# Two graph attention layers on one core: how the last batch's first layer hands over to its second

## The chip, the cores and the metric

The kernel runs on one core of one Trainium2 chip. The metric is the device time of one execution in microseconds (us); lower is better. The engines are named as in the profile: PE is TensorE, DVE is VectorE, ACT is ScalarE, POOL is GpSimd, and SP issues most of the DMA transfers. Each engine works through its own queue of instructions in a fixed order, and semaphores tie the queues together.

## The reference

The input is x, eight batches of 2048 nodes with 256 features in float32, and a 0/1 adjacency matrix of 2048 x 2048 that all batches share. Two layers follow one another; each ends with a residual sum and a normalization over the features:

```
# layer 0: attention in 4 heads of 64, softmax within chunks of 256 keys
q, k, v = x @ Wq.T + bq, x @ Wk.T + bk, x @ Wv.T + bv
scores  = clip(q . k / 8, -10, 10), and -10 where adj == 0
attn    = softmax(scores) over each chunk of 256 keys on its own
ctx     = sum over the 8 chunks of attn @ v
y       = layernorm(ctx @ Wo.T + bo + x) * gamma + beta
x1      = layernorm(x + y)

# layer 1: graph attention in 4 heads of 64
Wh      = x1 @ W
e       = leaky_relu(s_src[i] + s_dst[j], 0.2), masked by adj
h       = elu(softmax_j(e) @ Wh)
out     = layernorm(x1 + h)
```

## The kernel before, in words

**Layer 0.** A batch is worked through in four groups of 512 queries. For each group there are 16 *slots*: two pairs of heads times eight chunks of keys. So a batch has 64 slots, taken two at a time in 32 *pairs* (`p`). In a pair TensorE computes the next pair's scores (`unit`, L422), VectorE clips and masks them out of PSUM (`evict`, L439), ScalarE takes the exponential in place (`exps`, L462), and TensorE multiplies with the values and a column of ones (`product`, L473). ScalarE copies the product to SBUF (L480). `normalize` then divides by the sum: the reciprocal on VectorE (L490), a multiplication on GpSimd (L497), and from the second chunk on an addition to the head pair's sum, also on GpSimd (L499). A finished sum goes to DRAM and comes back turned; only the very last one of a batch is turned by TensorE (`context`, L523, with ScalarE's copy L526).

**Between the layers.** The class `Between` takes a group of 512 rows from its contexts to layer 1's inputs: output projection (L625), addition of the residual (L636), statistics and scaling for a first normalization ("a"), gamma (L642) and a second addition (`again`, L645), and statistics and scaling for a second one ("b"). Of each normalization, the statistics are on VectorE (`stats`, L540 to L549), the power and the offset on GpSimd (L550, L551), and the scaling on ScalarE (L588). The result, x1, is stored to DRAM (`finish`, L650). To be a matmul's weights it must be turned: `load` and `turn` read it back in blocks and transpose these on VectorE (L304, L322); `turn_all` does it with eight TensorE transposes and a copy by ScalarE (L331, L334). `values` projects it (L667). The groups of a batch pass through these steps while later pairs run, by tables that say after which part of which pair each step stands. Groups 2 and 3 of a batch come to their last steps after its last pair.

**Factors.** When all groups of a batch are projected, `factors` makes three pieces (`fs`): the maximum over nodes (L734 to L738), its spread and the exponentials (L742 to L756, of which L755 gives `ed`), and the rows of the source factor, which go through DRAM (L761 to L764), while GpSimd scales the projected values by `ed` in place (L765, L767).

**Layer 1.** The class `Layer1` works in units of 1024 queries and one head, eight to a batch, each with 16 *tiles* of 128 keys, so 128 tiles. `make` writes a tile of weights with one VectorE operation from a row, a column and a mask (L884); `use` multiplies it on TensorE (L913). At a unit's end ScalarE copies the sums (L925), and `close` finishes the unit in stages, one for each call of `rest` (L938 to L957). Masks come from DRAM by SP (L832), five tiles ahead.

**How they are interleaved.** Layer 1 of a batch runs beside layer 0 of the next: `along` is the earlier batch's `Layer1`, and every pair makes and uses four of its tiles. In the last batch (`b + 1 == B`) some tiles of the batch before are held back: from slot `SLOTS - LATE` on, pairs have none, and `step` (close a stage, then make and use two tiles) puts them between the steps of groups 2 and 3 after the last pair. The order in which these stand is a list written by hand (`order`, L1315 to L1319); there is no scheduler. Afterwards the last batch's layer 1 runs alone: its mask is loaded in whole (L798), its row is lifted to PSUM (L825), every third tile is made by ScalarE and GpSimd (L854 to L856), and the finished rows go out.

**Room.** Layer 1's tiles take turns in three buffers (`ep`), the probabilities of layer 0 in six (`prp`). In the last stage VectorE's tiles are in `prp` and the others in `ep`. Products, scores, turned blocks and projections take turns in three double banks of PSUM (`two_banks`).

Of the kernel before, what the change touches and what calls it, by code (L numbers as in the profile page):

```python
# [8 lines left out]
F32 = mybir.dt.float32  # L9
# [8 lines left out]
P = 128  # L18
# [4 lines left out]
def adj_resnorm_kernel(  # L23
# [19 lines left out]
    nc = tc.nc  # L43
# [29 lines left out]
    FIRST = [sum(BANKS[:m]) for m in range(len(BANKS))]  # L73
    TILES = len(UNITS) * NT
    STEP = TILES // SLOTS
    LATE = 18
    WIDE = max(BANKS)
    AHEAD_E = 5
    LEAD = 4
# [401 lines left out]
            raws[s].rearrange("p k i d -> p k (i d)"), pc[:, :, : QT * D1]  # L481
        )

    def normalize(s):

        q, hp, c = where[s]
        raw = raws.pop(s)
        del probs[s]
        rd = small.tile([P, 2, QT, 1], F32, tag="rd", name="rd")
        nc.vector.reciprocal(rd, raw[:, :, :, D:D1])  # L490
        if c == 0:
            accs[q, hp] = small.tile([P, QT, 2, D], F32, tag="acc", name="acc")
        accv = accs[q, hp].rearrange("p t k d -> p k t d")
        part = accv
        if c:
            part = small.tile([P, 2, QT, D], F32, tag="part", name="part", bufs=1)
        nc.gpsimd.tensor_mul(part, raw[:, :, :, :D], rd.to_broadcast([P, 2, QT, D]))  # L497
        if c:
            nc.gpsimd.tensor_add(accv, accv, part)  # L499

    sums = {}

# [273 lines left out]
    class Layer1:  # L776
        def __init__(self, b, gd, waug):
            self.b, self.gd, self.waug = b, gd, waug
            self.made = self.used = 0
            self.rows, self.edge, self.e = {}, {}, {}  # L780
            self.tail = []
            self.alone = b == B - 1
            self.masks = {}
            self.begun, self.lifted = 0, {}
# [74 lines left out]
        def make(self):  # L859

            if self.made == TILES:
                return
            k = self.made
            n, j = k // NT, k % NT
            _, h = UNITS[n]
            if j == NT // 2:
                self.load_row(n + 1)
            self.made += 1
            if not self.alone:
                drip()  # L870
                if j == 0:
                    need(("row", self.b, n))
                self.load_edge(k + AHEAD_E)
                e = ep.tile([P, WIDE * P], F32, tag="e", name="e")
                row = self.rows[n]
            else:
                if j == NT - LEAD:
                    self.lift(n + 1)
                self.make_ahead(k)
                if self.by_pool(k):  # L880
                    return
                e = prp.tile([P, WIDE * P], F32, tag="pr", name="e")
                row = self.lifted[n]
            nc.vector.scalar_tensor_tensor(  # L884
                e,
                row,
                self.gd[:, h, j : j + 1],
                self.mask(k),
                op0=ALU.max,
                op1=ALU.mult,  # L890
            )
            self.e[k] = e
# [261 lines left out]
    for b in range(B):  # L1154
# [6 lines left out]
        for p in range(PAIRS):  # L1161
            s0, s1 = 2 * p, 2 * p + 1
            q, i = p // QP, p % QP
            along = lower if b + 1 < B or s0 < SLOTS - LATE else None
            more = p + 1 < PAIRS
            slow[0] = bool(along) and more
            if not slow[0]:
                drip(len(pieces))

            def hook(now, later):  # L1170
                if group and i in now:
                    now[i](group)
                if before and i in later:
                    later[i](before)

            if p + 2 < PAIRS:
                load_slab(p + 2)
            if i == 0 and q:
                before, group = group, Between(b, q - 1, sd, waug)
            if p == PAIRS - 2 and b + 1 < B:  # L1180
                turns = [project(b + 1, g) for g in range(NCH)]
                turns[0].pop(0)()

            hook(FIRST_OF, {})
            if i == QP - 1 and q > 1:
                turn_context(q, 0)
            if p:
                normalize(s0 - 1)
            if more:
                us = units_of(p + 1)  # L1190
                waiting = burst(p + 1)
                evict(*waiting[0][0], waiting[0][1])
                exps(*us[0])
                exps(*us[1])
            if along:
                along.rest(1)
                along.make()
                along.use()
                along.make()
            else:  # L1200
                if more:
                    evict(*waiting[1][0], waiting[1][1])
                    exps(*us[2])
                if not lower and masks.left():
                    masks.step()
            hook(MIDDLE_OF, NEXT_MIDDLE)
            if closing:
                closing.do(p, "add", "factors")
            if i == 2 and q:
                turn_context(q - 1, 1)  # L1210
            if i == QP - 2 and q < 2:
                turn_context(q, 0)
            product(s0)
            send()
            if closing:
                closing.do(p, "load")
            if i == 1 and q:
                load_context(b, q - 1, 1)
            if i == QP // 2 + 1:
                load_context(b, q, 0)  # L1220
            if along:
                normalize(s0)
                if more:
                    for us_ps in waiting[1:]:
                        evict(*us_ps[0], us_ps[1])
            elif more:
                evict(*waiting[2][0], waiting[2][1])
                exps(*us[3])
            if i == 0 and q:
                send_context(b, q - 1, 1)  # L1230
            if i == QP // 2:
                send_context(b, q, 0)
            if along:
                if more:
                    exps(*us[2])
                along.rest(1)
                along.use()
                along.make()
                along.use()
                along.make()  # L1240
                along.use()
            else:
                normalize(s0)
                if not lower and masks.left() and (p < QP - 2 or p % 2 == 0):
                    masks.step()
            if p == PAIRS - 1:
                if b + 1 < B:
                    turns[0].pop(0)()
                group.again()
            product(s1)  # L1250
            if along and more:
                exps(*us[3])
            hook(LAST_OF, NEXT_LAST)
            hook(FINALLY_OF, NEXT_FINALLY)
            if closing:
                closing.do(p, "sums", "squares", "finish")
        normalize(SLOTS - 1)
        slow[0] = False

        send()  # L1260
# [3 lines left out]

        def begin():
            nonlocal group
            group = Between(b, NCH - 1, sd, waug)

        def ctx():
            context(NCH - 1, 1)  # L1270
# [6 lines left out]
        def start_next():  # L1277
            for us, ps in burst(0):
                evict(*us, ps)

        early = [
            lambda: before.b2.stats(every),
# [20 lines left out]
        if b + 1 < B:  # L1303
            (k0, v0, q0), (l1, t1, k1, v1, q1), (l2, t2, k2, v2, q2), (l3, t3, k3, v3, q3) = turns
            rest = [lambda: lower.rest(1)] if lower else []
            order = [begin, early[0], *rest, l1, k0, ctx, early[2], v0, steps[0], *rest, steps[1], t1, l2, *rest]
            order += [q0, steps[2], early[3], steps[3], l3, k1, *rest, steps[4], v1, early[4], t2, q1]
            order += [steps[5], k2, steps[6], early[5], early[6], steps[7], coming.begin, v2, t3]
            order += [lambda: [load_slab(p) for p in range(2)], steps[8], steps[9]]
            order += [lambda: k3(fs[0]), fs[1], lambda: q2(fs[2]), coming.start, v3, start_next]  # L1310
            order += [lambda: [exps(*us) for us in units_of(0)], q3, coming.make, coming.make]
        else:

            step = lower.step
            order = [begin, early[0], lambda: coming.load_masks(0), step, ctx, early[1], step, steps[0], steps[1], early[2], step]  # L1315
            order += [steps[2], step, steps[3], early[3], step, steps[4], step, steps[5], early[4], step]
            order += [steps[6], early[5], step, steps[7], early[6], step, steps[8], step, steps[9], step]
            order += [fs[0], step, fs[1], step, fs[2], coming.start]
            order += [step] * 5  # L1319
            assert sum(p is step for p in order) == LATE  # L1320
        for piece in order:
            send()
            piece()
# [63 lines left out]
```

## Time and profile before

| what | value |
|---|---|
| median of 3 runs | 3606.09 us (3604.92 to 3607.03) |
| the profiled execution's own time | 3600.65 us |
| its span | 3598.9 us |
| busy: PE, DVE, ACT, POOL | 3505.9, 3037.7, 2300.9, 1430.4 us |
| mean granted TensorE clock | 0.993 |

The span is the time from the first to the last instruction on record; the execution's own time has some 2 us more around it. A row of a group of instructions reads: line, engine, operation, what it writes and reads, the shapes, how often, and in a timeline ahead of this the start and the duration in us. What stands in brackets is how long the engine sat idle just before, and what ended that. In the span's time, the last batch's pairs with tiles end at 3262, its last pair starts at 3341, the last held tile is used up at 3426, and the last stage ends at 3586; some 13 us of closing work follow.

### The profile page before, as it was taken

The numbers are of one execution on the slowest core, as the hardware profiler recorded it, in microseconds if no ns is written. First come the engines' busy times: TensorE is split into PE (matmuls) and PEld (weight loads), VectorE is DVE, ScalarE is ACT, GpSimd is POOL, SyncE is SP. The second block draws the span as 40 slices with busy tenths as digits, with TensorE's granted clock in tenths as the row PEclk, the third lists the DMA queues.
The fourth block names the chain that finished last, engine by engine and source line by source line (L and its number), as shares of the span: only waits on it lengthen the run. The fifth ranks groups of instructions, "written<-read, shape, count | busy, mean of one in ns | idle before, by whom it ended". The sixth has DMA issues, their size and how long they took to land. (4 is left out here: it accounts for less than half of the span.)

```text
span 3598.9 us, 170175 instructions
## 1 busy us (share of the span) xinstructions
PE 3505.9 (97%) x76884; PEld 2611.6 (73%) x76884; DVE 3037.7 (84%) x3652; ACT 2300.9 (64%) x4119; POOL 1430.4 (40%) x1259
## 2 busy tenths in 40 slices
PE   8999999999999999999999999999999999998777
PEld 5666677777777777776777767777677777775677
DVE  5886699977999699996999959998699977996787
ACT  5787556665666566665666657666576666766376
POOL 1555234333333333333443424434343333344366
PEclk9999999999999999999999999999999999999999
DMA  7653333443443444443444344444344443443341
GB/s 177 152 131 81 84 99 101 111 103 103 116 108 103 90 127 109 112 103 88 126 109 103 99 105 126 111 102 99 101 120 108 111 102 105 116 109 78 103 126 38
DMA packets 724072, 386.58 MB, mean 107 GB/s; under 512 B 437264, under 2 KB 683408, under 8 KB 723344
## 3 DMA queue, kind: packets, MB, share of 16 engines
q1 hardware_dynamic: 673344, 342.00, 38.0%
q10 hardware_dynamic: 50000, 33.70, 2.9%
q8 instruction: 601, 9.85, 1.1%
q14 instruction: 127, 1.04, 0.1%
HBM read 318.64 MB, written 56.89 MB: 104 GB/s over the span
## 5 line engine op out<-in xcount | busy, mean ns | idle before, releaser
L462 ACT ACTIVATE pr<-pr 128x1024 f32<-128x1024 f32 x960 | 996.7, 1054 | 443.9 <-DVE pr L439 371.6
L439 DVE SCALAR_TENSOR_TENSOR pr<-ps,slab 128x1024 f32<-128x1024 f32 x960 | 1116.4, 1205 | 106.7 <-PE ps L422 84.8
L884 DVE SCALAR_TENSOR_TENSOR e<-srow,gd,et 128x1024 f32<-128x1024 f32 x896 | 1168.3, 1338 | 13.7 <-PE pa L913 8.6
L913 PEld LDWEIGHTS pa<-waug,e 128*64 128x64 f32 x32768 | 1008.9, 139 | 215.9 <-issue 166.7
L913 PE MATMUL pa<-waug,e 128*64 128x65 f32 x32768 | 1060.8, 224 | 39.8 <-DVE e L884 34.5
L473 PE MATMUL pc<-vaug,pr 128*64 128x65 f32 x30720 | 980.5, 222 | 10.0 <-DVE pr L439 9.7
L497 POOL TENSOR_TENSOR part<-raw,rd 128x512 f32<-128x512 f32 x448 | 476.7, 1064 | 1216.4 <-DVE rd L490 1212.1
L473 PEld LDWEIGHTS pc<-vaug,pr 128*64 128x64 f32 x30720 | 937.6, 138 | 28.7 <-DVE pr L439 25.8
L422 PE MATMUL ps<-qT,kT 64*64 64x512 f32 x8192 | 943.5, 596 | 5.9 <-DVE pr L439 3.3
L422 PEld LDWEIGHTS ps<-qT,kT 64*64 64x64 f32 x8192 | 286.5, 132 | 485.1 <-issue 269.3
L480 ACT COPY raw<-pc 128x520 f32<-128x520 f32 x512 | 302.6, 591 | 484.8 <-PE pc L473 482.2
L499 POOL TENSOR_TENSOR acc<-acc,part 128x512 f32<-128x512 f32 x448 | 587.2, 1311 | 35.2
L490 DVE RECIPROCAL rd<-raw 128x8 f32<-128x8 f32 x512 | 100.9, 197 | 134.0 <-ACT raw L480 127.1
L497 POOL TENSOR_TENSOR acc<-raw,rd 128x512 f32<-128x512 f32 x64 | 66.8, 1043 | 361.6 <-DVE rd L490 361.6
L667 PE MATMUL pw<-w_sb,x1T 128*64 128x264 f32 (+1 forms) x800 | 122.5, 386 | 4.1 <-DVE x1T L322 4.0
L366 PE MATMUL pp<-xT,wk_sb 128*128 128x512 f32 x256 | 118.4, 602 | 2.9 <-DVE xT L322 1.6
L625 PE MATMUL po<-wo_sb,qT 128*64 128x256 f32 (+1 forms) x912 | 120.7, 381 | 0.0
L366 PE MATMUL pp<-xT,wq_sb 128*128 128x512 f32 x256 | 117.4, 598 | 0.0
L949 ACT ACTIVATE sums<-sums,dn 128x64 f32<-128x64 f32 x448 | 117.0, 334 | 0.4 <-ACT y L588 0.4
L382 PE MATMUL pv<-wv_sb,xT 128*128 128x256 f32 x512 | 116.6, 381 | 0.0
L382 PEld LDWEIGHTS pv<-wv_sb,xT 128*128 128x128 f32 x512 | 95.9, 190 | 20.2 <-issue 7.2
L884 DVE SCALAR_TENSOR_TENSOR e<-rowp,gd,et 128x1024 f32<-128x1024 f32 x86 | 103.9, 1272 | 0.6 <-ACT rowp L825 0.6
(140 smaller groups left out, 2505.6 us busy)
## 6 DMA issues: line engine op xcount, KB each, us to landing
et<-edgeD SPq DMA_DIRECT2D x896, 128.0 KB, 2.8
slab<-clipD SPq DMA_DIRECT2D x256, 256.0 KB, 3.8
srow<-rowD SPq DMA_DIRECT2D x256, 128.0 KB, 3.6
xg<-in_x_dram SPq DMA_DIRECT2D x128, 128.0 KB, 3.3
x1D<-y ACTq DMA_DIRECT2D x32, 512.0 KB, 3.0
ctxD<-acc ACTq DMA_DIRECT2D x56, 256.0 KB, 3.4
ctx<-ctxD SPq DMA_DIRECT2D x224, 64.0 KB, 3.0
xp<-in_x_dram SPq DMA_DIRECT2D x224, 64.0 KB, 2.4
```

The lines of the kernel that those rows point to most:

```text
L366: nc.tensor.matmul(pps[c], lhsT=w[:, kc, c * P : (c + 1) * P], rhs=st["xT"][:, kc, :], start=(kc == 0), stop=(kc == KC - 1),)
L382: nc.tensor.matmul(pv[:, u, :], lhsT=st["xT"][:, kc, u * P : (u + 1) * P], rhs=wv_sb[:, kc, :], start=(kc == 0), stop=(kc == KC - 1),)
L422: nc.tensor.matmul(ps[z * D : (z + 1) * D, k, :], lhsT=kT[rows, hp, t * P + z * D : t * P + (z + 1) * D], rhs=qT[rows, hp, cols], start=Tr ...
L439: nc.vector.scalar_tensor_tensor(pr, ps, -CLIP, row.unsqueeze(1).to_broadcast([P, 2, CH]), op0=ALU.max, op1=ALU.min,)
L462: nc.scalar.activation(pr, pr, AF.Exp, scale=0.125)
L473: nc.tensor.matmul(pc[z * D : (z + 1) * D, k, to], lhsT=probs[s][u][:, k, i * P + z * D : i * P + (z + 1) * D], rhs=vaug[:, KT * c + u, 2 ...
L480: nc.scalar.copy(raws[s].rearrange("p k i d -> p k (i d)"), pc[:, :, : QT * D1])
L497: nc.gpsimd.tensor_mul(part, raw[:, :, :, :D], rd.to_broadcast([P, 2, QT, D]))
L499: nc.gpsimd.tensor_add(accv, accv, part)
L667: nc.tensor.matmul(pw[z, k, : F + 2 * H], lhsT=self.x1T[:, c, u * P + z.start : u * P + z.stop], rhs=w1_sb[:, c, :], start=(c == 0), stop= ...
L884: nc.vector.scalar_tensor_tensor(e, row, self.gd[:, h, j : j + 1], self.mask(k), op0=ALU.max, op1=ALU.mult,)
L913: nc.tensor.matmul(self.pa[i // QT][z * D : (z + 1) * D, i % QT, :], lhsT=e[:, i * P + z * D : i * P + (z + 1) * D], rhs=self.waug[:, j, h ...
```

## The change

All of it lies in the last batch. `LATE` goes from 18 slots to 12: pairs 23, 24 and 25 work beside four tiles each, as the pairs before them, and 24 tiles are held instead of 36. In the last pair the group object is created earlier, a tile is made ahead of gamma and another used between the two products, and `normalize` works on VectorE for the last two slots. After the last pair the list is a new one: single `make` (M), `use` (U) and `rest` (R) calls between the steps; group 2's x1 is turned with `turn_all`, so its `load` and `turn` are gone; group 3's addition of beta comes after its first statistics. Held tiles made there are in `prp`.

```diff
-    LATE = 18
+    LATE = 12
...
-    def normalize(s):
+    def normalize(s, engine=nc.gpsimd):
...
-        nc.gpsimd.tensor_mul(part, raw[:, :, :, :D], rd.to_broadcast([P, 2, QT, D]))
+        engine.tensor_mul(part, raw[:, :, :, :D], rd.to_broadcast([P, 2, QT, D]))
         if c:
-            nc.gpsimd.tensor_add(accv, accv, part)
+            engine.tensor_add(accv, accv, part)
...
+            self.room = ep, "e"
...
-                e = ep.tile([P, WIDE * P], F32, tag="e", name="e")
+                pool, tag = self.room
+                e = pool.tile([P, WIDE * P], F32, tag=tag, name="e")
...
+            ending = b + 1 == B and not more
+            if ending:
+                last = Between(b, NCH - 1, sd, waug)
...
+            if ending:
+                lower.make()
             hook(MIDDLE_OF, NEXT_MIDDLE)
...
+            elif ending:
+                lower.use()
+                group.again()
+                normalize(s0, nc.vector)
             else:
                 normalize(s0)
...
-            if p == PAIRS - 1:
-                if b + 1 < B:
-                    turns[0].pop(0)()
+            if p == PAIRS - 1 and not ending:
+                turns[0].pop(0)()
                 group.again()
             product(s1)
...
-        normalize(SLOTS - 1)
+        normalize(SLOTS - 1, nc.gpsimd if b + 1 < B else nc.vector)
...
-            group = Between(b, NCH - 1, sd, waug)
+            group = Between(b, NCH - 1, sd, waug) if b + 1 < B else last
...
-            step = lower.step
-            order = [begin, early[0], lambda: coming.load_masks(0), step, ctx, early[1], step, steps[0], steps[1], early[2], step]
-            order += [steps[2], step, steps[3], early[3], step, steps[4], step, steps[5], early[4], step]
-            order += [steps[6], early[5], step, steps[7], early[6], step, steps[8], step, steps[9], step]
-            order += [fs[0], step, fs[1], step, fs[2], coming.start]
-            order += [step] * 5
-            assert sum(p is step for p in order) == LATE
+            lower.room = prp, "pr"
+            M, U, R = lower.make, lower.use, lambda: lower.rest(1)
+            order = [begin, U, U, ctx, early[0], steps[0], steps[1], early[2], steps[2]]
+            order += [lambda: group.a.stats(every), before.turn_all, lambda: coming.load_masks(0)]
+            order += [group_shift, M, M, U, steps[4], early[5], U, early[6], M]
+            order += [steps[5], U, M, M, R, U, M, U, steps[6], R, steps[7], M, M, U, steps[8], R]
+            order += [U, steps[9], M, R, M, M, U, U, R, fs[0], M, U, fs[1], M, U, fs[2], coming.start]
+            done = sum(p is U for p in order) + 1, sum(p is M for p in order) + 1
+            order += [R, M, U] * (LATE * STEP - done[0])
+            assert LATE * STEP - done[0] >= LATE * STEP - 2 - done[1]
```

In this list `steps` are group 3's steps (bias, output, add, shift with statistics, a scaling, gamma with the second sum and its statistics, b scaling with the store, turn, and twice two blocks of projection), `early` those of group 2 that are left (statistics, nothing, b scaling with the store, load, turn, and twice two blocks of projection), and `fs` the three pieces of the factors.

More of the change, by code (lines that the diff above doesn't have):

```diff
@@ L1279, in start_next, with group_shift @@
                 evict(*us, ps)
+        def group_shift():
+            group.shift()
         early = [
```

## The prediction

> **What bounds the kernel now.** I read the page first. TensorE is busy nearly throughout, so only a stretch in which it idles can be shortened:
>
> ```profile
> PE 3505.9 (97%) x76884; PEld 2611.6 (73%) x76884; DVE 3037.7 (84%) x3652; ACT 2300.9 (64%) x4119; POOL 1430.4 (40%) x1259
> ```
>
> Then busy times by stretch, around the last batch's end. The columns are the stretch, its length, busy us of each engine, granted clock, DMA share, GB/s:
>
> ```profile
> 3262.25:3290.70 28.45, 23.90 (x483) 14.85 (x481) 18.31 (x22) 18.18 (x31) 10.32 (x9) 1.00 0.27 67
> 3346.72:3385.40 38.68, 24.45 (x512) 21.16 (x510) 33.29 (x57) 11.22 (x26) 13.11 (x10) 0.87 0.48 141
> 3385.40:3404.50 19.10, 18.48 (x439) 15.87 (x437) 15.09 (x21) 5.88 (x19) 0.04 (x1) 1.00 0.36 108
> 3404.50:3426.00 21.50, 13.86 (x333) 12.80 (x329) 18.96 (x14) 3.73 (x10) 11.39 (x5) 0.76 0.21 56
> 3426.00:3586.00 160.00, 131.30 (x4096) 128.55 (x4096) 133.42 (x172) 127.83 (x154) 116.79 (x69) 0.94 0.28 86
> ```
>
> The first row is pairs 23 to 25, without held tiles; rows two to four are the stretch with 36 held tiles, where TensorE works 56.8 of 79.3 us; the last is the last batch's second layer alone. TensorE's waits from 3343 to 3426 (us in all, times, longest) name the causes:
>
> ```profile
> PE pa L913 <- DVE e L884: 11.5, 6, 3.6
> PE pt L523 <- POOL acc L499: 6.3, 1, 6.3
> PE pw L667 <- DVE x1T L322: 4.0, 1, 4.0
> ```
>
> The timeline gives the durations. TensorE's score bursts show a pair with four tiles and a pair with none; GpSimd's rows are the last context; the VectorE and GpSimd rows from 3406 on show tiles made while GpSimd scales the weights:
>
> ```profile
> 3249.26 3.66 PE L422 MATMUL ps<-qT,kT 64*64 64x512 f32 x32
> 3262.25 3.66 PE L422 MATMUL ps<-qT,kT 64*64 64x512 f32 x32
> 3271.40 4.00 PE L422 MATMUL ps<-qT,kT 64*64 64x512 f32 x32 [0.18 <-DVE pr L439]
> ...
> 3350.66 2.11 POOL L497 TENSOR_TENSOR part<-raw,rd 128x512 f32<-128x512 f32 x1
> 3352.85 2.12 POOL L499 TENSOR_TENSOR acc<-acc,part 128x512 f32<-128x512 f32 x1
> ...
> 3404.15 0.26 ACT L755 ACTIVATE ed<-sd 128x64 f32<-128x64 f32 x1
> 3405.41 10.48 POOL L767 TENSOR_TENSOR waug<-waug,ed 128x1024 f32<-128x1024 f32 x4
> 3406.45 1.89 DVE L806 TENSOR_SCALAR ngd<-gd 128x64 f32<-128x64 f32 x1
> 3408.26 5.84 DVE L884 SCALAR_TENSOR_TENSOR e<-srow,gd,et 128x1024 f32<-128x1024 f32 x2
> ```
>
> The stretch is set by one chain: last context, output, two normalizations, x1, its projection, the factors (ed ends at 3404.4), the weights' scaling, the last held tiles. Held tiles only fill its gaps.
>
> **What the Trainium skill says.** SBUF — State Buffer, "SBUF: two separate sides": a VectorE operation with two SBUF inputs and a GpSimd operation that reads SBUF exclude each other for a whole instruction. The trace agrees: a tile costs 1.23 us alone and 2.92 beside the scaling. GPSIMD Engine Reference, "3.1 Elementwise": a GpSimd add takes 1.96 times VectorE's at 2048 elements; here L497 and L499 take 1.04 and 1.31 us undisturbed, 2.1 when tiles are made beside them. VectorE: DVE Perf Modes, "The three transpose paths": VectorE turns 32x32 blocks only, TensorE whole squares into PSUM. Here group 3 on TensorE takes 1.09 us and a 1.01 us copy, while group 2 goes through DRAM and needs L322.
>
> **The change, part by part.** Times are on the clock of the run before; its shift comes last.
>
> *Pairs 23 to 25 take four held tiles each.* Pairs with tiles and no extras last 11.21 us (scores at 3083.28 and 3094.49). Three cost 33.63 against 28.45 here, where TensorE idles 4.5 us. Pair 26's burst then follows matmuls at once (3.66 instead of 4.00 us): -0.3. **+4.8 us**, up to +5.8 if each lasts the longest such pair, 11.55.
>
> *Contexts on VectorE.* In pair 31 one tile is made ahead of gamma, but gamma waits for ScalarE (3345.83) anyway, so it is covered by an idle 3.38 us; uncovered it costs 1.23. TensorE uses a tile between the two products, which puts the second off by 0.95, to 3347.7; its copy comes at 3348.35, before VectorE asks for it at 3349.85. Gamma and the add end at 3348.25. Two reciprocals (0.2) and four operations of 512 elements follow. No row has these on SBUF; half of L642's 1.22 us for 1024 is 0.6, L636 reads PSUM at 0.69; I take 0.65 (0.4 to 1.0: -1 to +1.4 us in all). They end at 3351.5: the turn of the context (L523) starts there, not at 3355.03. Queued behind these are the b statistics of group 2; GpSimd, now free, has their factors at 3355.7, against 3357.2.
>
> *The chain without tiles in it.* Turn 1.11, copy 0.59, output 4.12 (3359.59 to 3363.71 before): 3357.4. Before, four tiles stood between copy and output, and two between output and add. Add 1.22, statistics 2.0: 3360.6, against 3372.7. Factors on GpSimd (1.0 to 2.0, plus 0.3) 3362.5, ScalarE 2.08 to 3364.6. VectorE makes shift and three tiles in that time (1.22 + 3.65): it is late, at 3365.45. Gamma, add, statistics 4.4: 3369.85, against 3381.9.
>
> *Group 2 on TensorE.* Removed: eight x1 loads on SP (4.95 us), L322 (1.25) and TensorE's 3.95 us idle. Added: eight turns (1.09, from 3357.8 on, when ScalarE has scaled y for 2.08 us after the factors) and a ScalarE copy (1.01), in the gap while VectorE finds group 3's statistics. TensorE then waits for tile 4 until 3363.1. If that cover were gone, 2 us would go on the chain. TensorE's queue (tile 4, projection, tile 5, projection, tile 6) ends at 3369.8, before tile 7 exists.
>
> *A wait that the order adds.* Group 3's second scaling now stands on ScalarE behind the two copies of unit 6's sums, which need tiles 7 and 8. VectorE makes these after the statistics (2.4 us: 3372.25), TensorE 1.3, copies 0.8, then 2.08: ready at 3376.3. Behind the copies stand this scaling, the x1 store, the x1 copy and the projections' copies, so the whole chain waits. By its factors alone it would be 2 to 3 us earlier. Still, before it was 3385.4.
>
> *To the factors.* From there: rest of the turn 0.65, tile 9 0.93 (the x1 copy runs beside it), projection 1.83, tile 10, projection, tiles 11 and 12 4.6: L736 starts 8.1 later. Before, L736 to the end of ed was 4.2 us with two tiles; with one it is 3.0. ed ends at 3387.5, not 3404.4: **-16.9 us**. The weights are unscaled until then, so nothing later moves ahead of it.
>
> *Scaling to the last held tile.* Both kernels have ngd, one h and eight tiles left on VectorE. Before it took 20.2 us, 2.3 of them waiting for L955, which stood behind the row's arrival; now L957 precedes it. By the lock: tile 16 1.2, one copy and four multiplications at 2.0 each, h 0.7, ngd 0.2, eight tiles at 1.23, nearly one after another: 19.4. **-0.8 us**, between -2.3 and +2.
>
> *At nothing.* The ring of six for tiles: scores are over. The mask load waits, as before, for the last product; one tile's mask load now goes ahead, and masks queued behind (the first for tile 9) have some 20 us. Group 3's residual was already loaded at 3329. The last stage has the same queues from the 24th tile on, so I carry its 160 us over; changed timing there may give or cost 3 us.
>
> The sum, 4.8 - 16.9 - 0.8 = -12.9, against the profiled execution: 3600.65 - 12.9 = 3587.8. The median is 5.4 above that execution, so 3606.1 - 12.9 = **3593**. Unknowns: VectorE's four operations (-1 to +1.4), lock and late factors (0 to +5), a TensorE clock that falls in gaps (it was 0.76 and 0.87; five restarts of up to 0.5 us: 0 to +2.5; TensorE: Matmul & The Clock Gate, "What's actually happening", says idleness lowers it), the last stage (3 either way). The likeliest case's own range is 3590 to 3598.
>
> **Rivals.** *Factors starved:* each of the three GpSimd power steps waits behind a burst of tiles. For it: tiles take the lock and now come in threes right after statistics. Against: before, with four tiles queued, one took 2.04 us only. Two steps late by 3.6 us (three tiles) lose 7: 3600.
>
> *The last stage gains too:* its unit ends idle TensorE by up to 5.1 us, and another phase against GpSimd may spare one: 3588. Against: same order, same entry.
>
> *Slower:* the last stage loses. At its first unit end (3445) the row lands late on SP behind 16 loads and TensorE waits 5.1 us. To pass +7.2 us overall it must lose 20, so four of seven unit ends must become that late: 3613. Nothing in the order moves those loads; only the timing could.
>
> *The change not doing what it says* is excluded: the built order shows fewer held tiles, four VectorE operations and no x1 loads.
>
> **How the numbers follow.** A difference of 0.2%, 7.2 us, is about what a measurement can tell from none. The main case has 0.62, the starved factors 0.17 (most of it within 7.2 us of before), the gaining last stage 0.14, the losing one 0.07. Faster: 0.62 + 0.14 + 0.04 = 0.80; same 0.13; slower 0.07. The range, 3587 to 3601, takes in the first three cases' centres and leaves the last out.
>
> **What would show it.** Right: pairs 23 to 25 at 11.2 us; L523 5.7 us after the last product's start, not 10.2; group 3's second scaling 9 us nearer to the last scores; ed 12 us earlier on the span's clock; the last held tile 19 to 20 us after ed; the last stage again 160 us. Wrong: a power step of 4 us or more, TensorE waiting over 3 us for single tiles many times, or a last stage off by more than 3 us.

## The result, and the profile after

The changed kernel takes 3591.97 us (median of 5 executions, 3591.74 to 3594.14) where the kernel before takes 3606.09 (5 executions, 3604.92 to 3610.02). The ratio is 0.9962, 95% interval 0.9952 to 0.9973: 14 us faster, between 10 and 17. A second measurement of both on another occasion, given below, has 0.9967 (0.9954 to 0.9979). The forecast was 3593.

The two profiled executions are only 8.1 us apart (3600.65 and 3592.51 us). Part of that is chance, as the first experiment shows; so the steps are compared by distances inside one execution, and for both kernels from two profiles each.

Stretches of the changed kernel's profile that answer to those of before, with the same columns: pairs 23 to 25; last context to group 3's second scaling; from there to the end of ed; from there to the start of the last stage; the last stage.

```profile
3264.23:3297.86 33.63, 33.63 (x867) 26.01 (x865) 32.40 (x36) 22.11 (x42) 12.67 (x11) 1.00 0.38 102
3353.43:3383.91 30.48, 21.46 (x341) 15.75 (x337) 26.53 (x54) 10.39 (x21) 6.90 (x7) 0.89 0.35 118
3383.91:3396.73 12.82, 12.76 (x235) 10.38 (x237) 7.27 (x13) 6.02 (x19) 0.00 (x0) 0.87 0.31 96
3396.73:3417.74 21.01, 15.55 (x332) 14.71 (x334) 20.30 (x13) 2.06 (x6) 11.99 (x5) 0.68 0.18 53
3417.74:3577.20 159.46, 134.54 (x4091) 132.01 (x4087) 132.13 (x168) 127.60 (x154) 116.88 (x69) 0.91 0.28 86
```

The pairs are filled to the last (33.63 of 33.63 us), and the held stretch, counted from 14.3 us after the last scores in both kernels, lasts 64.3 us, not 79.3. TensorE's waits in the changed kernel from 3350 to 3418:

```profile
PE pa L915 <- DVE e L886: 10.0, 5, 4.6
PE pt L523 <- DVE acc L499: 2.9, 1, 2.9
PE pt L331 <- ACT y L588: 1.5, 4, 1.0
```

The wait for the context fell from 6.3 to 2.9 us and the wait for L322 is gone; the 1.5 us for ScalarE's y are new. The wait for single tiles is about what it was (10.0 us for 11.5). Of the 10.0, 4.6 us lie ahead of ed, where the chain runs on beside them on other engines, and 5.4 after it, where the tiles themselves are what must be finished. For the kernel before, the start of the last scores and the turn of the last context are these lines:

```profile
3332.40 3.66 PE L422 MATMUL ps<-qT,kT 64*64 64x512 f32 x32
3355.03 1.11 PE L523 MATMUL pt<-identf,acc 128*128 128x128 f32 x4 [6.27 <-POOL acc L499]
```

In the changed kernel's timeline the instructions of this stretch, in order of time:

```profile
3339.11 3.66 PE L422 MATMUL ps<-qT,kT 64*64 64x512 f32 x32
3349.11 2.20 DVE L886 SCALAR_TENSOR_TENSOR e<-srow,gd,et 128x1024 f32<-128x1024 f32 x1
3352.58 2.08 DVE L642 TENSOR_TENSOR y<-y,gamma_sb 128x1024 f32<-128x1024 f32 x1 [1.26 <-ACT y L588]
3357.70 0.69 DVE L497 TENSOR_TENSOR part<-raw,rd 128x512 f32<-128x512 f32 x1
3358.43 0.69 DVE L499 TENSOR_TENSOR acc<-acc,part 128x512 f32<-128x512 f32 x1
3359.26 0.63 PE L523 MATMUL pt<-identf,acc 128*128 128x128 f32 x4 [2.86 <-DVE acc L499]
3359.82 5.67 PE L625 MATMUL po<-wo_sb,qT 128*64 128x256 f32 x32
3368.83 1.92 POOL L550 TENSOR_TENSOR rs_a<-rs_a,nhalf 128x4 f32<-128x4 f32 x1 [5.52 <-DVE off_a L549]
3381.10 0.84 ACT L927 COPY sums<-pa 128x260 f32<-128x260 f32 x2 [2.04 <-PE pa L915]
3381.84 2.07 ACT L588 ACTIVATE y<-y,off_b,rs_b 128x256 f32<-128x256 f32 x4
3386.45 2.77 PE L667 MATMUL pw<-w_sb,x1T 128*64 128x264 f32 x16
3396.47 0.26 ACT L755 ACTIVATE ed<-sd 128x64 f32<-128x64 f32 x1
3398.36 16.29 DVE L886 SCALAR_TENSOR_TENSOR e<-srow,gd,et 128x1024 f32<-128x1024 f32 x8
```

The last scores start at 3339.11 and ed ends at 3396.73: 57.6 us, where before it was 72.0. The eight tiles after it take 16.29 us, and not the 9.8 of eight tiles at 1.23 us: GpSimd's scaling runs beside them.

### The profile page after: what moved, and what is told of

It reads as the page before. It is cut to its first block, busy times and chain, and to the rows that moved or that the text cites. A ratio compares the mean times of both kernels' runs of the same rounds, so it can differ in the third digit from the quotient of the medians.

```text
span 3590.6 us, 170172 instructions
## 1 busy us (share of the span) xinstructions
PE 3512.4 (98%) x76892; PEld 2619.9 (73%) x76892; DVE 3040.5 (85%) x3655; ACT 2302.9 (64%) x4120; POOL 1424.7 (40%) x1255
## 3 DMA queue, kind: packets, MB, share of 16 engines
q14 instruction: 127, 1.04, 0.1%
## 4 chain that ended last, share of the span: by engine, by line
PE 86%; DVE 7%; issue 2%; DMA 2%; ACT 1%; POOL 1%; SPq 0%; DVEq 0%; ACTq 0%; POOLq 0%
PE pa L915 24%; PE pc L473 23%; PE ps L422 23%; PE pp L366 6%; PE po L625 3%; PE pv L382 3%; PE pw L667 3%; DVE e L886 3%; DVE pr L439 2%; POOL acc L499 1%; DMA et<-edgeD 1%; DVE h L439 0%; POOL part L497 0%; ACT e L855 0%; PE pm L270 0%
## 5 line engine op out<-in xcount | busy, mean ns | idle before, releaser
L497 POOL TENSOR_TENSOR part<-raw,rd 128x512 f32<-128x512 f32 x446 | 473.7, 1062 | 1221.3 <-DVE rd L490 1217.2
L422 PE MATMUL ps<-qT,kT 64*64 64x512 f32 x8192 | 942.3, 596 | 5.5 <-DVE pr L439 3.2
L422 PEld LDWEIGHTS ps<-qT,kT 64*64 64x64 f32 x8192 | 287.3, 132 | 482.5 <-issue 270.1
L499 POOL TENSOR_TENSOR acc<-acc,part 128x512 f32<-128x512 f32 x446 | 583.9, 1309 | 35.1
L497 POOL TENSOR_TENSOR acc<-raw,rd 128x512 f32<-128x512 f32 x64 | 66.8, 1044 | 361.1 <-DVE rd L490 361.1
```

The source lines that it names most:

```text
L422: nc.tensor.matmul(ps[z * D : (z + 1) * D, k, :], lhsT=kT[rows, hp, t * P + z * D : t * P + (z + 1) * D], rhs=qT[rows, hp, cols], start=Tr ...
L497: engine.tensor_mul(part, raw[:, :, :, :D], rd.to_broadcast([P, 2, QT, D]))
L499: engine.tensor_add(accv, accv, part)
```

## Experiments

Times are medians, each beside the kernel before run on the same chip. That kernel's own median was between 3603.96 and 3607.47 us on these occasions, so two rows are compared by their ratios, a thousandth of which is 3.6 us. "To ed" is the time from the start of the last scores (the last L422 burst) to the end of L755 in the profile; "to the stage" is from there to VectorE's first tile of the last stage.

| run | time, us | ratio to before (95%) | to ed | to the stage |
|---|---|---|---|---|
| before | 3606.09 | - | 72.0 | 20.1 |
| before, again | 3602.35 | 0.9998 (0.9990 to 1.0006) | 74.3 | 20.3 |
| changed | 3591.97 | 0.9962 (0.9952 to 0.9973) | 57.6 | 17.8 |
| changed, again | 3591.29 | 0.9967 (0.9954 to 0.9979) | 56.6 | 17.8 |
| contexts on GpSimd | 3594.45 | 0.9972 (0.9963 to 0.9982) | 61.0 | 17.8 |
| x1 through DRAM | 3594.22 | 0.9974 (0.9964 to 0.9984) | 60.2 | 17.8 |
| both back | 3596.56 | 0.9972 (0.9961 to 0.9982) | 61.1 | 17.8 |
| old list, 24 tiles | 3601.61 | 0.9996 (0.9987 to 1.0004) | 66.8 | 20.5 |
| new list, 36 tiles | 3605.69 | 1.0003 (0.9995 to 1.0011) | 58.0 | 36.8 |
| new list, 20 tiles | 3590.61 | 0.9961 (0.9948 to 0.9973) | 58.6 | 12.5 |
| new list, 16 tiles | 3582.81 | 0.9939 (0.9927 to 0.9951) | 56.4 | 9.8 |
| scaling ahead of sums | 3589.75 | 0.9958 (0.9946 to 0.9971) | 55.2 | 17.8 |

The theory is that of the prediction: the chain through the contexts, two normalizations, x1 and the factors sets the stretch, and a held tile costs only where it stands on that chain or after it.

**The kernel before, once more.** No edit.

> The kernel before, unchanged, as a measure of what two copies of one kernel differ by. The two profiled executions are 8.1 us apart (3600.65 and 3592.51) while the medians are 14.1 us apart. Theory: the profiled execution of before was one of its shortest, by chance in the long middle part; then this run's executions lie at 3605 +- 3 and a new profile may show a span of 3599 to 3608. Rival: the profile itself makes this kernel 5 us shorter; then the new profiled execution is again near 3600 and the timed ones near 3606.

Thirteen executions lay between 3598.4 and 3605.6 us, and the profiled one took 3604.11. So the execution of before that the forecast started from was one of its shortest; the profile does not shorten it. Two places differ. Pair 23's burst starts at 3262.25 and 3262.79, so the middle part is alike here (in the changed kernel it was 3264.23 and 3264.56, although the edit touches nothing up to there; more of this in the next section); and in the second execution TensorE worked slowly after its wait for x1. The first line is of the first profile of before, the second of this one:

```profile
3383.40 2.00 PE L667 MATMUL pw<-w_sb,x1T 128*64 128x264 f32 x16 [3.95 <-DVE x1T L322]
```

```profile
3384.09 3.79 PE L667 MATMUL pw<-w_sb,x1T 128*64 128x264 f32 x16 [3.87 <-DVE x1T L322]
```

The same instruction in the same place after the same wait takes 2.00 us or 3.79. So single profiles of this stretch differ by some 2 us by themselves, and a step of less must not be read from one.

**Contexts back on GpSimd.**

```diff
-                normalize(s0, nc.vector)
+                normalize(s0)
...
-        normalize(SLOTS - 1, nc.gpsimd if b + 1 < B else nc.vector)
+        normalize(SLOTS - 1)
```

> The changed kernel with the last two slots' division back on GpSimd. Theory (the last context stands on the chain): L523 starts 1.5 to 3.5 us later against the last product, and the time is 2 to 3 us above the changed kernel's, near 3594. Rival (covered by other work): no difference, 3592.

TensorE waits for the last context 5.7 us instead of 2.9, in this line of its timeline:

```profile
3361.49 1.12 PE L523 MATMUL pt<-identf,acc 128*128 128x128 f32 x4 [5.67 <-POOL acc L499]
```

From the last scores to this turn it is 22.97 us, not 20.15, and ed comes 3.3 and 4.4 us later than in the two profiles of the changed kernel. By the ratios the kernel is 1.8 to 3.6 us slower than the changed one. The place is shown by the trace; the times alone, with intervals that overlap, would not settle it.

**Group 2's x1 through DRAM again.**

```diff
-            order += [lambda: group.a.stats(every), before.turn_all, lambda: coming.load_masks(0)]
-            order += [group_shift, M, M, U, steps[4], early[5], U, early[6], M]
+            order += [lambda: group.a.stats(every), early[3], lambda: coming.load_masks(0)]
+            order += [group_shift, M, M, U, steps[4], early[4], early[5], U, early[6], M]
```

> The changed kernel with group 2's x1 stored, read back and turned on VectorE, as before. Theory: the projection of group 2 waits for the round trip, about 6 us, and TensorE's queue behind it (tiles 5 to 8, then the sums, then group 3's scaling) is late by most of that: 4 to 7 us above the changed kernel, 3596 to 3599. Rival (hidden in the gap while group 3's statistics are found): within 1 us of it.

The wait is there, on both engines, but it is smaller than was expected. VectorE's and TensorE's timelines of this kernel:

```profile
3374.52 1.25 DVE L322 STREAM_TRANSPOSE x1T<-x1t 128x1024 f32<-128x1024 f32 x1 [2.33 <-DMA x1t<-x1D]
```

```profile
3375.91 3.79 PE L667 MATMUL pw<-w_sb,x1T 128*64 128x264 f32 x16 [2.86 <-DVE x1T L322]
```

Group 3's second scaling starts 4.0 and 3.7 us later against the last scores than in the two profiles of the changed kernel, ed 2.6 and 3.7 later; the first projection behind it ran at 2.00 us here and at 2.77 and 2.00 there, which is the spread seen above. By the ratios it is 2.5 to 4.3 us. That is at most the lower end of the expected 4 to 7 us: the round trip had been put at 6 us and cost 3 to 4.

**Both back.** The two edits above together.

> The changed kernel with both parts undone: the last two contexts on GpSimd and group 2's x1 through DRAM; 24 held tiles and the new list stay. Alone they put ed off by 3.3 and 2.6 us against the last scores. Theory (each is on the chain on its own): 5 to 6 us later, ed at +63 to +64 us from the last scores against +57.6, and about 5 us above the changed kernel. Rival (the later context gives the round trip more time, so one hides the other): 3.3 to 4 us later.

ed comes 3.5 and 4.5 us later than in the two profiles of the changed kernel, hardly more than with either alone, as the rival had it, and the ratio is that of either alone. With the later context VectorE reaches group 2's turn 36.4 us after the last scores, when the blocks have landed; in the run before it waited 2.3 us for them, until 35.2. TensorE's wait for L322 is 0.4 us here and was 2.9. So the two parts overlap: against the means of the two profiles they are worth 3.9 and 3.2 us on the chain singly and 4.0 together.

**The old list with 24 tiles.** The kernel before with `LATE = 12`, six of its double steps left out ahead of the factors.

```diff
-            order = [begin, early[0], lambda: coming.load_masks(0), step, ctx, early[1], step, steps[0], steps[1], early[2], step]
-            order += [steps[2], step, steps[3], early[3], step, steps[4], step, steps[5], early[4], step]
-            order += [steps[6], early[5], step, steps[7], early[6], step, steps[8], step, steps[9], step]
+            order = [begin, early[0], lambda: coming.load_masks(0), ctx, early[1], step, steps[0], steps[1], early[2]]
+            order += [steps[2], step, steps[3], early[3], steps[4], step, steps[5], early[4]]
+            order += [steps[6], early[5], step, steps[7], early[6], step, steps[8], steps[9]]
```

> The kernel before with 24 held tiles instead of 36, its own list less six of its double steps, five still standing after the factors. Theory A (the placement of single tiles and the new order make the gain): pairs 23 to 25 cost 4.7 us, of the chain only 4 to 6 us go, so within 3 us of before. Theory B (VectorE's tiles on the chain make it: twelve tiles at 1.23 us are 14.8 us): the chain shortens by 10 to 12 us, net 6 to 8 us below before, at least half of the whole gain.

It is 0.04% from before (0.9987 to 1.0004): fewer held tiles alone bring nothing that the times show. Twelve tiles with 14.8 us of VectorE's work are off the stretch, and ed comes 5.3 to 7.6 us nearer to the last scores, of which the three pairs take 4.7. TensorE's waits in this kernel from 3348 to 3426 tell where the rest went:

```profile
PE pw L667 <- DVE x1T L322: 12.5, 1, 12.5
PE pa L913 <- DVE e L884: 8.7, 5, 3.6
PE pt L523 <- POOL acc L499: 7.5, 1, 7.5
```

The old list has group 2's turn on VectorE behind group 3's second statistics, and group 2's projection on TensorE ahead of tiles that could run. With 36 tiles TensorE reached that projection 4.0 us too early, with 24 tiles 12.5. So the twelve tiles were only in part a burden there, and otherwise filled a wait of the list. (Which six double steps go was chosen; another choice was not tried.) In the new list (and with the edit's smaller parts in the last pair), also with 24 tiles and with both other parts undone, ed is at 61.1 us, 5.7 nearer than here, and the ratio is 0.9972 (0.9961 to 0.9982) for 0.9996 here: intervals that do not meet, some 9 us. The new list is thus shown as the part without which the fewer tiles, so chosen, are worth nothing.

What the list owes to its order alone is not shown, for its tiles also have six buffers instead of three. VectorE waits 8.6 us for a free buffer in the stretch of the kernel before, once with the addition of the residual (L636, on the chain) right behind it, though TensorE had the output ready at 3363.9:

```profile
3364.86 1.28 DVE L884 SCALAR_TENSOR_TENSOR e<-srow,gd,et 128x1024 f32<-128x1024 f32 x1 [2.85 <-PE pa L913]
3366.06 1.22 DVE L636 TENSOR_TENSOR y<-po,xg 128x1024 f32<-128x1024 f32 x1
```

In the old list with 24 tiles it is 9.9 us, there with the addition waiting for TensorE in any case; with the new list, in the kernel with both parts back as in the changed one, it is nothing. The new list with three buffers was not run.

**The number of held tiles in the new list.** The further uses, or the missing ones, are those after the factors.

```diff
-    LATE = 12
+    LATE = 18
...
+    LATE = 10
...
+    LATE = 8
```

> The changed kernel with 36 held tiles again; the twelve more stand at its list's end, after the factors. Theory (a held tile after the factors costs VectorE's 1.23 us in full): three pairs get 4.7 us shorter, twelve tiles add 14.8, and the sums of a unit now end at the 4th tile, ahead of group 3's first scaling, which adds 2: about 12 us above the changed kernel, near 3604. Rival (held tiles fill idle time for nothing): 4.7 us below it, 3587.

> The changed kernel with 20 held tiles (pair 26 works beside tiles as well). Theory: +1.6 us for the pair, -4.9 for four tiles fewer after the factors, +2.5 for the sums that now stand ahead of group 3's first scaling, -1.4 since none stand ahead of its second: 1 to 3 us below the changed kernel, 3589 to 3591. Rival (24 is the optimum, because the row's way through DRAM and GpSimd's scaling need the cover of ten tiles): 1 to 3 us above it.

> The changed kernel with 16 held tiles, just the last unit; two of them are left after the factors. Theory: +3.2 us for two pairs, -1.4 for the sums gone from the chain, and the last stage starts when GpSimd has scaled the weights and the row has arrived, 11 to 12 us after ed instead of 20: 5 to 7 us below the changed kernel, 3585 to 3587. Rival (the ten tiles cover work that must be waited for anyway): TensorE stands idle for what was covered, and with +3.2 it ends 1 to 3 us above it.

With 36 tiles ed stays where it was (58.0), the twelve tiles come after it, and the last stage starts 36.8 us after ed instead of 17.8. That is 19 us for twelve tiles, 4 more than 14.8: one tile of them waits for its mask, which stands on SP behind the row, in VectorE's timeline:

```profile
3409.04 1.28 DVE L886 SCALAR_TENSOR_TENSOR e<-srow,gd,et 128x1024 f32<-128x1024 f32 x1 [4.12 <-DMA et<-edgeD]
```

The new list with as many tiles as before is no faster than before. So what the list brings, the tiles after the factors take back: the change needs both parts.

With 20 tiles the stage starts 5.3 us sooner after ed, with ed 0.9 to 2.0 us later; the pair with tiles, put at 1.6 us, costs 2.3 (12.97 us for 10.63), and the last pair 0.3. The median is 1.4 us lower, but the ratio, 0.9961, cannot be told from the changed kernel's 0.9962 and 0.9967. With 16 tiles it is 3582.81 us, by the ratio some 8 us below the changed kernel (9 on one chip, below), where 5 to 7 were expected. The two pairs cost 4.6 us, not 3.2, so by the terms that were named it would have been about 4; the rest is in the last stage. In the timeline after the factors:

```profile
3399.53 0.26 ACT L755 ACTIVATE ed<-sd 128x64 f32<-128x64 f32 x1
3400.80 7.52 POOL L767 TENSOR_TENSOR waug<-waug,ed 128x1024 f32<-128x1024 f32 x4
3408.58 1.02 ACT L826 COPY rowp<-srow 128x1024 f32<-128x1024 f32 x1 [8.50 <-DMA srow<-rowD]
3409.63 2.48 DVE L886 SCALAR_TENSOR_TENSOR e<-rowp,gd,et 128x1024 f32<-128x1024 f32 x2 [8.73 <-ACT rowp L826]
3411.06 11.84 PE L915 MATMUL pa<-waug,e 128*64 128x65 f32 x320 [9.16 <-DVE e L886]
```

TensorE now idles 9.2 us, for the row's way through DRAM, and yet the time is lower: eight tiles after ed had cost more than the wait that they covered. Undisturbed by tiles, GpSimd's scaling takes 7.52 us, where it took 11.03 beside them. What had not been expected is in the last stage: from VectorE's first tile to the last product it is 158.0 us, in the changed kernel 162.6 (and 161 before). The first tile from GpSimd comes 2.9 us after VectorE's first, and 5.5 in the changed kernel. ScalarE's part of it stands behind the copies of the last held unit's sums, and these wait for a TensorE that is behind (2.00 us for a tile after each gap). That this is the whole of the 4.6 us was not tested.

**The wait that the order adds.** The eighth tile's use moved behind the second scaling.

```diff
-            order += [steps[5], U, M, M, R, U, M, U, steps[6], R, steps[7], M, M, U, steps[8], R]
+            order += [steps[5], U, M, M, R, U, M, steps[6], U, R, steps[7], M, M, U, steps[8], R]
```

> The changed kernel with the eighth tile's use put behind group 3's second scaling, so that the scaling is ahead of the two copies of sums on ScalarE. Theory (the added wait of the prediction): the scaling starts when its offset is there (3380.4 in the changed kernel's trace) and not at 3381.8, so 1.3 us off the chain, less than a time can show; the distance from the last scores to ed falls from 57.6 to 56 or 56.5 us. Rival (TensorE has tile 8 later and the turn still waits): no shorter.

The scaling starts 41.4 us after the last scores instead of 42.7, as soon as its offset is there, which is the 1.3 us expected; ScalarE's line names the offset as its releaser:

```profile
3380.51 2.08 ACT L588 ACTIVATE y<-y,off_b,rs_b 128x256 f32<-128x256 f32 x4 [0.89 <-POOL off_b L551]
```

ed is at 55.2, 2.4 and 1.4 us sooner than in the two profiles of the changed kernel. The 1.3 us are in the trace; in the time (3589.75) they cannot be told from chance.

**16 tiles, six used after the factors.**

```diff
-            order += [U, steps[9], M, R, M, M, U, U, R, fs[0], M, U, fs[1], M, U, fs[2], coming.start]
+            order += [U, steps[9], M, R, M, M, M, M, R, fs[0], fs[1], fs[2], coming.start, U, U, U, U]
```

> 16 held tiles, of which six are made before the factors and used after them, so that TensorE's 9 us of waiting for the row are filled and no tile stands between the last projection and the factors. Theory (the factors are the chain, the row's way through DRAM follows them): L736 0.8 to 1 us and ed 1.5 us earlier against the last scores than with 16 held tiles (+54.9 instead of +56.4), and the time 1 to 2 us below it. Rival (L736 waits for ScalarE's copy anyway and the tile fills the wait): no difference in ed.

3582.68 us, the same as with 16 tiles. ed is at 55.4, 1.0 and 0.6 us sooner than in the two profiles with 16 tiles, and L736 only 0.4 and 0.1; less than single profiles can tell. The last stage is 1.8 us longer than in the first of these (159.8 for 158.0). In the place of the tile VectorE waits, with an earlier unit's h queued ahead of the maximum (its timeline):

```profile
3396.51 0.69 DVE L959 SCALAR_TENSOR_TENSOR h<-ee,sums 128x512 f32<-128x512 f32 x1 [1.43 <-ACT sums L957]
3397.12 0.21 DVE L734 TENSOR_REDUCE top<-sd 128x4 f32<-128x64 f32 x1
```

The same h stands there with 16 tiles. So a third thing stood in that gap, which both the theory and its rival had left out.

**Changed and 16 tiles once more, on one chip.**

> The changed kernel, unchanged, beside the kernel before and the one with 16 held tiles on one chip, since its first measurement had five executions. Theory: the change is worth 12 to 14 us, a ratio of 0.9961 to 0.9967, and its distance from the last scores to ed is 57.6 us within the 2.3 us by which two profiles of the kernel before differ. Rival (the first measurement had a low draw, and the profiles' 8.1 us are the effect): a ratio of 0.9975 to 0.9980.

> 16 held tiles again, beside the changed kernel. Theory: 6 to 9 us below it, a ratio to before of 0.9937 to 0.9945. Rival (the first measurement was on a quicker chip): within 4 us of it.

3591.29 and 3581.86 us beside 3604.41: ratios 0.9967 (0.9954 to 0.9979) and 0.9935 (0.9921 to 0.9949). The change is worth 13 to 14 us by these two pairs of medians, and 16 held tiles beat both kernels, by 9 us and by 22 to 23. "To ed" was 56.6 and 56.1 us.

## Why the prediction was right

Its sum was +4.8 - 16.9 - 0.8 = -12.9 us. From the means of two profiles of each kernel the terms are +4.7, -16.1, -2.4 and, for the last stage that was put at 0, +1.3: -12.5. With the ratio's 10 to 17 us and the second measurement's 13 that agrees.

This leaves out the part ahead of pair 23, which is 1.9 us longer in the two profiles of the changed kernel; with it the four profiles differ by 10.6 us, so the medians show some 3 us more than the profiled executions, which the interval allows. Whether the 1.9 us are chance is open: in all eleven profiles of kernels with the new list pair 23 starts at 3263.0 to 3265.1 us, in the three of the old list at 3262.2 to 3262.8.

The forecast number, 3593, also took the median to lie 5.4 us above the profiled execution. That holds for before, whose profiled execution was a short one; in the changed kernel the two agree (3591.97 and 3592.51). So the two profiles taken alone show 8.1 us, and the right number rests on the pairing of a profile with its own median.

The mechanism was right, but that the sum came so close is in part luck. The working had ed 55.1 us after the last scores, and it came at 57.6 and 56.6, 1.5 to 2.5 us late; the -16.1 above owes 1.2 us to the second profile of the kernel before, whose ed was 2.3 us later than the one worked from. The stretch from ed to the last stage made up for it, 1.6 us shorter than said and just outside its range. The terms:

- **Pairs 23 to 25.** 33.63 us, as worked out. From pair 23's start to the last scores it is 74.88 us, 70.15 before: +4.7 for +4.8.
- **Contexts.** The turn came 20.15 us after the last scores, 22.63 before: 2.5 us sooner, not 3.5. The cover failed in part: the tile ahead of gamma took 2.20 us and gamma 2.08, beside GpSimd's L497 and L499 of the slot before, so that the step called free cost 0.9 us. Gamma itself did not start later: VectorE idled 1.26 us ahead of it. But the tile held up GpSimd's multiplication (L497, 1.91 us for 1.04), so that GpSimd's addition fell on gamma. The four operations took 0.69 us each, for 0.65 assumed. The experiment put the part at 2.8 us at the turn.
- **The chain without tiles.** From the turn's start to the output's end it was 6.2 us, for 5.8 by the working. The output took 5.67 us where 4.12 had been taken from a TensorE at work, but it began before the copy was through, and the turn took 0.63 and not 1.11. The 0.4 us belong to the restarts, put at 0 to 2.5 us in all. Statistics, gamma and the second addition took what was said, and TensorE's wait for tile 4 was 4.6 us (4.4 by the working).
- **Factors.** Each power step took 1.92 to 2.03 us, the upper of the two values in the trace. None waited behind a burst of tiles; that rival is out.
- **Group 2 on TensorE.** Right in kind, the projection no longer waits for L322. Its own worth is 2.6 to 3.7 us, and with the contexts 3.5 to 4.5 for both; the prediction had not said that the two overlap.
- **The added wait.** 1.3 to 1.5 us, for the 2 to 3 of the working. The second scaling was ready 44.8 us after the last scores; the working had 43.9.
- **To the factors.** L736 to ed took 3.0 us, as said. From the scaling's end to L736 it was 9.8 us in one profile and 8.4 in the other, for 8.1: in the first a tile took 2.00 us and the projection 2.77, in the second 1.15 and 2.00.
- **Scaling to the last held tile.** 17.8 us, not 19.4. The step's items, as listed, add up to 21 and not to 19.4 (1.2, 1.0 for the copy, four times 2.0, 0.7, 0.2 and 9.84); the overlap behind "nearly" had no number. The two engines did hold each other up as the step has it, 16.29 us for eight tiles instead of 9.84 and 11.03 for four multiplications instead of 7.52, but ngd and h ran beside GpSimd's copy and not between its multiplications. TensorE then lost 1.2 us of it again, being behind VectorE at the end.
- **The last stage.** Put at 0, within 3 either way: +1.3.
- **At nothing.** The ring of six was put at nothing; no run separates it from the list, as said above.
- **The signs named beforehand.** Pairs of 11.21 us came as said. L523 came 6.8 us after the last product's start, for 5.7; the second scaling 8.2 us nearer to the last scores, for 9; ed 7.7 us earlier on the span's clock, for 12 (11.3 in the second profiles). No power step took 4 us, and TensorE waited over 3 us for a single tile once.

What the prediction did not ask is whether ten tiles after the factors were too many. It counted the 19.4 us from ed as given in both kernels, because both have ten tiles there; the trace had the row at hand 10.7 us after ed and the weights scaled at 11.5.

## What to carry to other kernels

Work that is held back to fill gaps helps only in gaps that something else has made: after the factors twelve held tiles cost 19 us, four 5.3 and eight 8.0, so 1.0 to 1.6 us each, around VectorE's own 1.23. The test is to hold fewer and see the idle time come back without the time growing. When two ways of shortening a chain are measured singly, undo both at once too; here they were worth 3 to 4 us each and about 4 together. And before a profile of one execution is compared with a profile of another, profile the same kernel twice: at one instruction 2 us came and went here without an edit.

## What the runs showed of the hardware that was not expected

- The same projection of 16 matmul records, after the same wait of 3.9 us, took 2.00 us in one execution of one kernel and 3.79 in another.
- VectorE's gamma product (two SBUF inputs) took 2.08 us beside GpSimd's work, 1.22 alone; GpSimd's four weight multiplications took 7.52 us without tiles beside them, 11.03 with.
- The power step on 128x4 elements took 1.0 us or about 2.0, the longer time where VectorE made tiles or a sum of two SBUF tiles beside it.
- From the store of the row to DRAM (L764) to its copy on the other side (L826) it was 8.1 us in the changed kernel, 8.5 with 16 held tiles and 7.4 with six of them used late. With 16 held tiles this way sets the start of the last stage, though barely: GpSimd's scaling had ended 0.3 us before the row's copy began.
